# Four-layer graph network, 64 graphs: the plan's account of PSUM changed from half banks to whole banks, and the order made anew

## The chip, the cores and the metric

The kernel runs on one core of one Trainium2 chip. A core has a matrix engine (TensorE, PE in the profile, with its weight loads shown apart as PEld), three elementwise engines (VectorE = DVE, ScalarE = ACT, GpSimd = POOL) and a sync engine (SP), which here issues every DMA. Matrix products land in PSUM, of which this program holds eight tiles of 128 x 512 float32, one bank each. The metric is the device time of one execution in microseconds (us).

## The reference, cut to what matters

There are 64 graphs of 256 nodes with 256 features in float32. Each goes through four layers in turn, and after each layer `x = layernorm(x + layer(x, adj))`:

```
layer 0: X,q,k = leaky_relu(x@W) in 4 heads;  A = adj * sigmoid(q k^T), scaled by degree^-1/2 on both sides
         out = layernorm(A @ X)
layer 1: 8 heads of masked softmax attention, then @ Wo
layer 2: agg = eps*x + adj @ x;  h = silu(rmsnorm(agg @ W1 + b1))   (W1: 256 x 1024)
         out = h @ W2 + b2                                           (W2: 1024 x 256)
layer 3: Wh = x @ W;  softmax over masked leaky_relu(s1_i + s2_j);  out = gelu(layernorm(att @ Wh))
```

The graphs are independent of each other. Within a graph each layer waits for the one before.

## The kernel before, in words

The program is fully unrolled and its order is made by a planner written in Python, which runs while the kernel is built. `graph()` lists the work of one graph as operations (`op(engine, cost, fn, writes, reads, ...)`). A `Value` is a buffer; its letter says where it lives: `s`, `d`, `b`, `c` are SBUF buffers of several sizes, `h` lies in DRAM, and `p` is one PSUM bank. The slots of each kind are limited (`SLOTS`: 42 of `s`, 8 of `p`, and so on). A `Value` may have parts: most PSUM values have two, the two halves of the bank (columns 0 to 255 and 256 to 511). An operand written `(ps, 0)` names one half, a bare `ps` names all.

`Plan.order()` then schedules all operations of all 64 graphs against a table of costs. It picks, among the operations whose predecessors are placed, the one with the earliest start; ties go to the one that is due first. Three things besides data bear on the choice:

- `AHEAD`: an operation without predecessors (a load from DRAM) may be placed only when the current turn is within `AHEAD` turns of the turn in which its result is due. Turns are the stretches in which ScalarE keeps one table of functions; a graph passes four of them per round, and there are 272 in all.
- `STAY`: when PE has just run products that use a part of the array's rows or columns (`mode="rows"`: L444 and L524; `mode="columns"`: L462, L484 and L560), a candidate of another mode has its start raised by `STAY` nanoseconds in the comparison, so that PE stays in the mode while it can. Everything else is `full` or `transpose`.
- `CHANGE` and `AFTER`: the planner's own prices of a change of mode and of a hand-over between engines.

The operations are then emitted in the order of their planned starts (`emit`), and a layer below puts in the semaphores: an instruction waits for the earlier-emitted instructions whose buffers it touches. The planner's parts decide the order; they do not set the semaphores. Each engine runs its instructions strictly in the emitted order.

The names that the later sections use, with their lines in the kernel before: 

- L603: the hidden layer of layer 2. `agg` is multiplied with `W1`; each bank takes two operations on PE, one per half (`[(ps, i)]`), 256 banks in all. L608 and L610 are ScalarE's readers of each half: the square for the norm (`sq`) and the scaled copy (`hT`). L615 adds the squares on DVE.
- L645: the second product of layer 2; L591: the product with the adjacency; L637: its Silu.
- L320 and L331: the plain projections (`feature_major`, `token_major`), each two operations for a bank. The query projection of layer 1 is read half by half at L510 (ScalarE); the attention product of layer 3 (L331 `ps<-v,eT`) is read half by half by the statistics at L345 (DVE).
- L524: the scores of layer 1, four banks in one operation; L407 (DVE) and L412 (ScalarE) are their softmax. L444 to L484 are layer 0's scores, degrees and product.
- L545, L287 with L547, L549, L293 to L301: transposes through DRAM, issued on SP.

Of the kernel before, what the change touches and what calls it, by code (L numbers as in the profile page):

```python
# [27 lines left out]
DMA_KB, DMA_SEEN = 4, 1900  # L28

WORDS = {"s": 516, "d": 1024, "b": 2048, "c": 32, "p": 512, "h": 1024}  # L30
AHEAD = 14
STAY = 200
NEAR = 1, 1, 3

ROUND = 0, 2, 5, 7
# [43 lines left out]
class Plan:  # L79
# [7 lines left out]
        self.graph = 0  # L87

    def op(self, engine, cost, fn, w=(), r=(), turn=None, mode="full", after=None, size=0):
        pair = lambda x: x if isinstance(x, tuple) else (x, None)  # L90
        w, r = [pair(x) for x in w], [pair(x) for x in r]
        op = Op(engine, cost, fn, w, r, self.graph, turn, mode, after, size)
        op.table = turn is not None and engine == "ACT"
        if op.table:
            self.turns[turn] = self.turns.get(turn, 0) + 1
        self.ops.append(op)

    def order(self):
# [13 lines left out]
        while ready:  # L112
            best = None
            for op in ready:
                if (op.due - AHEAD if op.first else op.turn or 0) > turns[turn]:
                    continue
                start = clock[op.engine]
                if op.engine == "PE" and mode in ("rows", "columns") and mode != op.mode:
                    start += STAY - 60 * (op.mode == "transpose")
                start = max(start, op.ready)  # L120
# [15 lines left out]
            _, start, op = best  # L136
            op.start = start
            ready.discard(op)
            if op.table and op.turn != loaded:
                op.start, loaded = op.start + TABLE_LOAD, op.turn  # L140
# [5 lines left out]
            if op.engine == "SP":  # L146
                moved = max(moved, end) + op.size * DMA_KB
                op.landed = max(op.landed, moved + DMA_SEEN)
            self.busy[op.engine] += op.cost
            done.append(op)  # L150
            op.takes = [v for v in op.values if v.slot is None]
            for v in op.takes:
# [26 lines left out]
def weights(plan, nc, c, t):  # L179
# [10 lines left out]
    def weight(name, key, rows=D, cols=D):  # L190
        v = const(name, [P, rows // P, cols])
        op("SP", 420, lambda: nc.sync.dma_start(
            v.t, t[key].rearrange("(k p) f -> p k f", p=P)), [v], after=3500, size=rows * cols // 256)
# [580 lines left out]
```

## Time and profile before

| | us |
|---|---|
| median of 3 runs (2766.03 to 2769.21) | 2768.54 |
| the profiled execution | 2761.13 |
| its span, first to last instruction | 2759.3 |
| PE busy | 2703.5 |
| PEld busy | 2160.5 |
| DVE busy | 2443.0 |
| ACT busy | 2224.2 |
| POOL busy | 574.6 |

Busy times overlap between engines. A PE product of 128 x 256 is shown with 379 ns, but a stream of them starts one every 216 ns (the timeline has 32 of L603 in 7.17 us), so PE can be shown as busy while it stands behind its best pace by up to 163 ns. The granted clock was 0.996. A time "waited for" is idle time of the waiting engine ahead of an instruction, put down to the event that ended it.

### The profile page before, as it was taken

To read this page: it belongs to the slowest core of one execution; us is meant where nothing else is said; L and a number is where in the kernel's file an instruction comes from. 1 tells how busy PE (TensorE), PEld (TensorE's weight loads), DVE (VectorE), ACT (ScalarE), POOL (GpSimd) and SP (SyncE) were. 2 spreads that over 40 slices of the span, in tenths; PEclk is the share of its full clock that TensorE was granted. 3 is DMA by queue.
4 is the path that set the end of the run, shared out by engine and by line. 5 is a ranking of instruction groups with operands and counts; after the bars stand their busy time and mean duration, and the time that the engine had idled before them with its cause. 6 is when DMAs were issued, how large, how long until landed. Compare 5 with 4: busy or idle time off the path is not lost.

```text
span 2759.3 us, 56034 instructions
## 1 busy us (share of the span) xinstructions
PE 2703.5 (98%) x17280; PEld 2160.5 (78%) x17280; DVE 2443.0 (89%) x7426; ACT 2224.2 (81%) x5323; POOL 574.6 (21%) x902
## 2 busy tenths in 40 slices
PE   8999999999999999999999999999999999999997
PEld 6778777777777777787877877788778777777776
DVE  6989998898898889989989989889989899899966
ACT  4878888778788888788878887888888887888775
POOL 1112222122121121221221212212212122122212
PEclk9999999999999999999999999999999999999999
DMA  5677677676677566766756756757667677576651
GB/s 157 199 210 198 172 204 201 176 205 167 193 215 191 157 192 173 211 176 189 210 161 190 217 158 195 211 152 209 184 176 212 166 189 218 143 206 188 184 135 35
DMA packets 710923, 505.17 MB, mean 183 GB/s; under 512 B 310112, under 2 KB 669920, under 8 KB 710624
## 3 DMA queue, kind: packets, MB, share of 16 engines
q1 hardware_dynamic: 710624, 501.59, 65.9%
q8 instruction: 138, 2.26, 0.3%
q14 instruction: 161, 1.32, 0.2%
HBM read 303.44 MB, written 197.92 MB: 182 GB/s over the span
## 4 chain that ended last, share of the span: by engine, by line
PE 75%; DVE 10%; ACT 6%; DMA 4%; SPq 2%; issue 2%; POOL 0%; DVEq 0%; POOLq 0%; ACTq 0%
PE ps L331 13%; PE ps L320 13%; PE ps L645 13%; PE ps L603 11%; PE ps L444 4%; PE ps L524 4%; PE ps L484 3%; PE av L560 3%; PE ps L660 3%; PE ps L591 3%; ACT e L412 2%; DVE e L407 2%; DVE st L345 1%; DMA eT<-far 1%; PE ps L275 1%
## 5 line engine op out<-in xcount | busy, mean ns | idle before, releaser
L412 ACT ACTIVATE e<-e,low 128x256 f32<-128x256 f32 x1152 | 579.8, 505 | 87.5 <-DVE low L407 86.6
L645 PE MATMUL ps<-w,hT 128*128 128x256 f32 x2048 | 478.8, 383 | 5.5 <-ACT hT L637 4.8
L603 PE MATMUL ps<-aggT,w 128*128 128x256 f32 x2048 | 476.4, 382 | 3.8 <-DVE low L407 1.9
L357 POOL TENSOR_SCALAR mv<-mv 128x2 f32<-128x2 f32 x384 | 123.0, 320 | 1573.3 <-DVE mv L347 1012.1
L645 PEld LDWEIGHTS ps<-w,hT 128*128 128x128 f32 x2048 | 382.4, 191 | 68.1 <-issue 6.7
L603 PEld LDWEIGHTS ps<-aggT,w 128*128 128x128 f32 x2048 | 379.7, 190 | 69.4 <-DVE low L407 11.7
L407 DVE CUSTOM_DVE_ANT_0 e<-ps,adj 128x256 f32<-128x256 f32 x1024 | 361.1, 420 | 12.7 <-PE ps L524 11.2
L545 DVE STREAM_TRANSPOSE eb<-e 128x1024 f32<-128x1024 f32 x252 | 306.2, 1224 | 9.3 <-ACT e L412 9.2
L608 ACT ACTIVATE sq<-ps,b 128x256 f32<-128x256 f32 x512 | 242.0, 480 | 82.7 <-PE ps L603 73.0
L358 POOL TENSOR_TENSOR mv<-mv,mhalf 128x2 f32<-128x2 f32 x384 | 298.6, 778 | 32.0
L610 ACT ACTIVATE hT<-ps,br,r 128x256 f32<-128x256 f32 x512 | 288.8, 575 | 10.2 <-PE ps L645 6.7
L372 ACT ACTIVATE x<-y,mv 128x256 f32<-128x256 f32 x384 | 217.3, 602 | 50.9 <-DVE mv L368 48.9
L345 DVE BATCH_NORM_STATS2 st<-y 128x6 f32<-128x256 f32 x640 | 245.2, 413 | 0.9
L412 ACT ACTIVATION_READ_ACCUMULATOR e<-e,low 128x1 f32 x1152 | 225.4, 196 | 0.0
L615 DVE TENSOR_TENSOR sq<-sq 128x512 f32<-128x512 f32 x192 | 131.0, 682 | 98.1 <-ACT sq L608 97.2
L450 DVE TENSOR_TENSOR att<-att,adjT 128x512 f32<-128x512 f32 x256 | 166.6, 681 | 5.1 <-ACT att L448 5.1
L524 PE MATMUL ps<-kT,qT 32*128 32x256 f32 x2048 | 152.0, 400 | 4.3 <-ACT kT L311 4.2
L635 DVE TENSOR_TENSOR hT<-hT,pr 128x1024 f32<-128x1024 f32 x128 | 149.7, 1209 | 5.3 <-PE pr L631 5.3
L470 POOL TENSOR_TENSOR dp<-dp,mhalf 128x8 f32<-128x8 f32 x64 | 106.8, 1668 | 196.3 <-DVE dp L469 166.2
L448 ACT ACTIVATE att<-ps 128x512 f32<-128x512 f32 x256 | 132.2, 603 | 5.6 <-PE ps L444 3.0
L637 ACT ACTIVATE hT<-hT 128x1024 f32<-128x1024 f32 x128 | 128.9, 1050 | 9.1 <-DVE hT L635 7.9
L524 PEld LDWEIGHTS ps<-kT,qT 32*128 32x128 f32 x2048 | 97.9, 184 | 47.5 <-issue 23.3
(113 smaller groups left out, 5486.0 us busy)
## 6 DMA issues: line engine op xcount, KB each, us to landing
far<-eb SPq DMA_DIRECT2D x252, 512.0 KB, 3.8
eT<-far SPq DMA_DIRECT2D x1008, 128.0 KB, 3.9
adj<-in_adj SPq DMA_DIRECT2D x128, 256.0 KB, 4.6
far<-eb SPq DMA_DIRECT2D x488, 64.0 KB, 1.8
x0T<-in_xT SPq DMA_DIRECT2D x64, 256.0 KB, 3.6
adjT<-in_adjT SPq DMA_DIRECT2D x64, 256.0 KB, 4.4
x<-in_x SPq DMA_DIRECT2D x64, 256.0 KB, 4.8
adj<-in_adjT SPq DMA_DIRECT2D x64, 256.0 KB, 5.4
```

The costliest lines, as they stand in the source:

```text
L320: pe.matmul(two(ps)[:, o, :], w.t[:, k, o * P:(o + 1) * P], two(xT)[:, k, :], start=(k == 0), stop=(k == DB - 1))
L331: pe.matmul(two(ps)[:, n, :], two(xT)[:, k, n * P:(n + 1) * P], w()[:, k, :], start=(k == 0), stop=(k == DB - 1))
L345: op("DVE", 328, lambda n=n: dve.bn_stats(st.t[:, 6 * n:6 * n + 6], two(src)[:, n, :]), [(st, n)], [(src, n)])
L358: pool.tensor_tensor(m()[:, :, 2], m()[:, :, 2], c.mhalf[:, :NB], OP.pow)
L407: op("DVE", 345, lambda n=n: dve.tensor_tensor_reduce(out=E(n), in0=two(logits)[:, n, :], in1=two(negmask)[:, n, :], scale=-scale, scalar= ...
L412: op("ACT", 491, lambda n=n: act.activation(E(n), E(n), AF.Exp, bias=low.t[:, n:n + 1], scale=-1.0, accum_out=r.t[:, col(n):col(n) + 1]), ...
L524: pe.matmul(two(pss[i])[:, n, :], two(qT1)[s, hq, n * P:(n + 1) * P], two(kT1)[s, hq, :], start=True, stop=True)
L545: op("DVE", 1155, lambda e=e, eb=eb: dve.transpose(eb.t.rearrange("p (b g i) -> p g b i", b=4, i=32), e.t.rearrange("p (g b i) -> p g b i" ...
L603: pe.matmul(two(ps)[:, i, :], c.w2_1.t[:, k, (j + i) * P:(j + i + 1) * P], two(aggT)[:, k, :], start=(k == 0), stop=(k == DB - 1))
L608: op("ACT", 357, lambda ps=ps, sq=sq, i=i, j=j: act.activation(two(sq)[:, i, :], two(ps)[:, i, :], AF.Square, bias=c.b2_1.t[:, j + i:j + i ...
L610: op("ACT", 491, lambda ps=ps, i=i, j=j: act.activation(Hb(j + i)[:, 0], two(ps)[:, i, :], AF.Identity, bias=c.br2.t[:, j + i:j + i + 1], ...
L645: pe.matmul(two(ps)[:, n, :], Hb(j)[:, 0, n * P:(n + 1) * P], c.w2_2.t[:, j, :], start=(j == 0), stop=(j == HB - 1))
```

## The change

In the planner a part of a PSUM value no longer counts: an operand of kind `p` always stands for the whole bank. So in the plan a reader of either half comes after the products of both halves, and a product into the second half never comes after a reader of the first. Two constants go with it: `AHEAD` from 14 to 12, `STAY` from 200 to 250. `graph()` itself, the operations and the prices are the same; line numbers in the changed file are one higher from the edit on.

```diff
-AHEAD = 14
-STAY = 200
+AHEAD = 12
+STAY = 250
...
     def op(self, engine, cost, fn, w=(), r=(), turn=None, mode="full", after=None, size=0):
-        pair = lambda x: x if isinstance(x, tuple) else (x, None)
+
+        pair = lambda x: (x[0], None if x[0].kind == "p" else x[1]) if isinstance(x, tuple) else (x, None)
         w, r = [pair(x) for x in w], [pair(x) for x in r]
```

Because every choice of the planner depends on the ones before, the order of all five queues is new from near the start on. The number of instructions on each engine is the same in both.

## The prediction

> **What bounds the kernel now.** I read the head of the page first: which engine is full, and whose work the chain of waits is made of.
>
> ```profile
> span 2759.3 us, 56034 instructions
> PE 2703.5 (98%) x17280; PEld 2160.5 (78%) x17280; DVE 2443.0 (89%) x7426; ACT 2224.2 (81%) x5323; POOL 574.6 (21%) x902
> PE 75%; DVE 10%; ACT 6%; DMA 4%; SPq 2%; issue 2%; POOL 0%; DVEq 0%; POOLq 0%; ACTq 0%
> ```
>
> PE sets the end. DVE and ACT have slack, and count only where PE stands for them. So the question is how much PE stands, and where. The busy times by stretch (span, then PE, PEld, DVE, ACT, POOL) say where:
>
> ```profile
> 0.00:100.00 100.00, 92.27 (x618) 71.60 (x619) 68.02 (x203) 61.55 (x145) 15.48 (x24) 0.98 0.47 145
> ...
> 1300.00:1600.00 300.00, 298.12 (x1911) 239.37 (x1911) 268.39 (x816) 248.09 (x595) 61.51 (x98) 1.00 0.68 187
> ...
> 2620.00:2759.30 139.30, 114.25 (x602) 94.48 (x600) 91.86 (x279) 92.55 (x202) 26.21 (x49) 0.93 0.35 88
> ```
>
> PE is idle 55.8 us (2759.3 - 2703.5): 7.7 us in the first 100 us, 25.1 us in the last 139 us, of which 16.5 us follow its last product (the final norms). The 2520 us between hold only 23.0 us (the nine stretches there, with 2497.0 us busy). That is all a better order can show as idle in the steady state. Besides, PE loses time inside "busy" where products follow each other more slowly than every 216 ns, above all around the tiled modes. PE's timeline (start, duration) shows the price of one:
>
> ```profile
> 1486.78 1.89 PE L645 MATMUL ps<-w,hT 128*128 128x256 f32 x8
> 1488.60 2.00 PE L444 MATMUL ps<-qT,kT 64*128 64x256 f32 x16
> 1490.52 3.72 PE L645 MATMUL ps<-w,hT 128*128 128x256 f32 x16
> 1494.08 0.38 PE L669 MATMUL ps<-ident,v 128*128 128x128 f32 x2
> ```
>
> Going in: 1.82 us for eight products, against 8 x 0.216 = 1.73, is 0.09 more. The block takes 1.92 us where eight pairs at 0.216 make 1.73: 0.19 more. The 16 products after it take 3.56, against 3.46: 0.10 more. A lone tiled block thus costs 0.38 us over the bare products.
>
> Last, how the halves of a bank behave today. From the timelines of PE and ACT around one hidden layer:
>
> ```profile
> 103.05 7.07 PE L603 MATMUL ps<-aggT,w 128*128 128x256 f32 x32
> ```
>
> ```profile
> 104.98 0.47 ACT L608 ACTIVATE sq<-ps,b 128x256 f32<-128x256 f32 x1 [0.96 <-PE ps L603]
> ```
>
> Four instructions make a half. The first half was complete at about 104.1 (three pitches of 0.216 and one duration of 0.38), the whole bank at 103.05 + 7 x 0.216 + 0.38 = 104.94. ACT, idle for 0.96 us, started at 104.98: it waited for the **whole bank**, though it reads half. And the other way round:
>
> ```profile
> 448.55 0.48 ACT L608 ACTIVATE sq<-ps,b 128x256 f32<-128x256 f32 x1 [0.51 <-DVE xb L383]
> ...
> 449.28 0.57 ACT L610 ACTIVATE hT<-ps,br,r 128x256 f32<-128x256 f32 x1
> ...
> 449.90 1.99 PE L603 MATMUL ps<-aggT,w 128*128 128x256 f32 x8 [1.66 <-ACT hT L610]
> ```
>
> PE stood 1.66 us until ACT had read the first half, before it wrote the second. So the semaphores already keep a bank to one engine; only the planner thinks in halves.
>
> **What the Trainium skill says.** "PSUM — Partial Sum Buffer", section "PSUM bank collisions raise a hardware error", has two engines on one bank and the same partitions at once as an error, at different columns too, and the rule to guard by bank; the two waits above agree that this program is guarded so. "TensorEngine Tiling (Array Packing)", "Key Properties", says that a change of tiling mode drains TensorE; the 0.09 and 0.10 us above agree. "Perfetto Trace Analysis", "Identifying the Most-Contended Engine", warns that the busy share of products does not measure distance to the best; the 0.38 us hidden in a 100% busy stretch agrees.
>
> **The change part by part.** No instruction is added or removed (17280 on PE, and the same issues on SP); the order of all queues, SP's and POOL's among them, is new. I counted in the two orders.
>
> (a) Tiled blocks. `STAY` 250 keeps PE longer in a mode. Runs of L444/L524 fall from 182 to 173, runs of L462/L484/L560 from 115 to 105. A merged block saves the way in and the way out, 0.09 + 0.10, and at most the whole 0.38: 19 x 0.19 = 3.6 to 19 x 0.38 = 7.2 us, all on PE's path. I take **-4**.
>
> (b) Second halves placed behind a reader of the first: 21 banks before (17 of L603, 4 of L331), none after. At four of these places PE's pitch shows the loss: 1.83 us at 449.90, 0.29 at 670.03, 0.18 at 2556.35, 0.22 at 2667.07 (pitch less the usual one). **-2.5**, with 0 as the other bound, if PE then stands for the next thing.
>
> (c) Readers planned too early. At the other 239 banks of L603, the 64 of the query projection and 60 of layer 3 the plan starts the reader when half a bank is done; the real one stands for the other half, 0.86 us of products on. The waits of before show it on ACT and DVE:
>
> ```profile
> DVE sq L615 <- ACT sq L608: 97.2, 73, 4.6
> ACT e L412 <- DVE low L407: 86.6, 65, 4.8
> ACT sq L608 <- PE ps L603: 73.0, 72, 2.9
> ACT qT L510 <- PE ps L320: 24.5, 23, 3.2
> DVE st L345 <- PE ps L331: 23.5, 27, 2.5
> ```
>
> In the new order ACT has other work there. These 121 us (73.0 + 24.5 + 23.5) lie beside PE's work and are not 121 us of gain; they matter as far as late ACT and DVE work makes PE stand later. PE's middle idle time without (b) is about 21 us; by PE's list of waits most of it ends on ACT or DVE. I take a third of it, **-7**; bounds 0 and -21.
>
> (d) Banks held longer. A half no longer frees its reader, and other work slips between the halves more often: banks whose halves aren't adjacent on PE go from 209 to 273 (L603: 31 to 67). Such a bank stays taken meanwhile, and PE may find none of the eight free. The nearest row is L603 standing for DVE L407 (which frees banks): 13.6 us in 34 waits, 0.4 us each, and 0.16 hidden, 0.56. That hit 34 of 256 banks, 13%: 64 x 13% x 0.56 = 5; below, 0; if all 64 stood, 36. I take **+2**.
>
> (e) `AHEAD` 12. A turn is 2759 / 272 = 10.1 us, so a load is issued about 20 us later, still some 120 us ahead of use. Loads land in 3.6 to 5.4 us (the page's DMA issues): nothing, covered by the lead itself; on SP they now stand behind more of the transposes' issues. It frees `s` buffers (live ones in order of emission: peak 42 of 42 before, 41 after), so no load waits for a slot; too small to price.
>
> (f) Start and end. The first 28 PE operations are nearly the same, the last 40 nearly so, and the drain after them is the same chain: 0, with +-4 as bounds.
>
> Sum: -4 - 2.5 - 7 + 2 = -11.5 us. Against the profiled execution's own 2761.1 that is 2749.6. That execution was 7.4 us quicker than the median of the runs shown (2768.5), so on the median I expect **2757**.
>
> **The rivals.** *The stalls only move.* PE's waits (c) come from a greedy order's accidents and return elsewhere; only (a) stays, some of it spent on (d): -4 + 2, 2766.5. For it: PE idles only 23 us in 2520, and ACT's waits cost little now. Against: (b) is a plain loss that goes. Much the same holds if the edit doesn't do what it says: real banks were never shared, so nothing is protected that was not. *The banks become the bound, slower.* One mechanism: half-filled banks held across other work (d), with no gain from (c). If 30 of the 64 further split banks make PE stand 0.56 us, that is +16.8 against -6.5: +10.3, 2779. It decides from about 21 such waits on ((6.5 + 5.5) / 0.56). For it: DVE L407 ends already more of L603's idle time than any other releaser. Against: a split is chosen because another product was ready, so PE works meanwhile. *The plan now fits the machine.* All of the 21 us of (c) goes, with (a) and (b): -27.5, 2741. For it: ACT's and DVE's waits above are the model's error made visible. Against: PE also stands for transfers and for true chains.
>
> **How the numbers follow.** A measurement of this kernel can tell about 0.2%, 5.5 us, from no change. Likeliest case 0.48, with the larger gain 0.13: faster 0.61. Stalls only move: 0.16. Slower: 0.23. The range runs from 2736 (the large gain, with the upper bound of (a) and of (f)) to 2780 (the bank rival).
>
> **What would show it.** Right: ACT L608's wait for PE L603 falls from 73 us to below 25; no PE wait on ACT L610 ahead of an L603; about 253 instead of 279 ways from full or transpose into tiled products; PE's idle time between 100 and 2620 us near 14 instead of 23. Wrong: PE standing for DVE L407 well beyond the 13.6 us at L603 (then the banks bind), or PE idle as long as before while ACT's waits are gone (then they never mattered).

## The result, and the profile after

| | before | after |
|---|---|---|
| median of 5 runs each, us | 2766.7 (2763.5 to 2769.2) | 2746.95 (2742.6 to 2752.1) |
| the profiled execution, us | 2761.13 | 2746.95 |
| its span, us | 2759.3 | 2745.2 |

The ratio is 0.9928, with a 95% interval of 0.9912 to 0.9945: 19.75 us less in the medians. The two profiled executions differ by 14.2 us, because the one of before was a quick one.

The head of the page after:

```profile
span 2745.2 us, 55992 instructions
...
PE 2690.7 (98%) x17280; PEld 2172.4 (79%) x17280; DVE 2442.3 (89%) x7426; ACT 2222.4 (81%) x5323; POOL 567.8 (21%) x902
```

PE is idle for 2745.2 - 2690.7 = 54.5 us, against 55.8 before. Of the 14.1 us of span only 1.3 are idle time; 12.8 came out of PE's *busy* time, though PE runs the same 17280 products. So nearly all of the gain lies in time that the page shows as busy. The busy times by stretch (span, then PE and the other engines) say the same:

```profile
0.00:100.00 100.00, 90.63 (x585) 68.70 (x586) 63.10 (x187) 58.98 (x139) 14.21 (x22) 0.97 0.44 137
...
1300.00:1600.00 300.00, 297.82 (x1934) 239.75 (x1933) 272.62 (x836) 248.08 (x600) 62.63 (x98) 1.00 0.71 192
...
2605.90:2745.20 139.30, 115.11 (x606) 96.18 (x604) 90.71 (x282) 89.66 (x201) 25.82 (x50) 0.93 0.35 92
```

Start (9.4 us idle against 7.7) and end (24.2 against 25.1) are as before, and between 100 us and the last 139 us PE idles 21.0 us against 23.0. The waits of ACT and DVE that the change was to shorten (waiting engine and line, releaser, us, times, longest):

```profile
ACT e L413 <- DVE low L408: 75.8, 42, 4.0
DVE sq L616 <- ACT sq L609: 75.1, 63, 5.4
...
ACT qT L511 <- PE ps L321: 33.0, 25, 4.2
...
ACT sq L609 <- PE ps L604: 27.1, 46, 2.9
...
DVE st L346 <- PE ps L332: 9.2, 11, 2.0
```

Line numbers are one higher than before. ACT's wait for the hidden layer's banks fell from 73.0 to 27.1 us; the query projection's, which is the same kind of bank, rose from 24.5 to 33.0; DVE's for layer 3's attention product fell from 23.5 to 9.2. The three together fell from 121.0 to 69.3 us.

**What hides in "busy".** Two blocks of layer 1's scores in PE's timeline of the kernel before (start, duration):

```profile
128.15 1.15 PE L524 MATMUL ps<-kT,qT 32*128 32x256 f32 x16
129.22 0.28 PE L567 MATMUL ps<-ident,r 128*16 128x128 f32 x1
129.34 1.89 PE L331 MATMUL ps<-w_o,yT 128*128 128x256 f32 x8
131.16 1.56 PE L524 MATMUL ps<-kT,qT 32*128 32x256 f32 x16
132.66 1.99 PE L320 MATMUL ps<-x0T,w_q 128*128 128x256 f32 x8
```

The same 16 products took 1.07 us from start to the next start in one place and 1.50 in the other. No idle time is noted, since an instruction is always in flight. I therefore compared, for all 17280 products of each profile, the time to the next start with the pitch of that place in its block where nothing is waited for (the lower quartile over all profiles of this study). What lies next to or within tiled blocks at that best pace, over the bare products, I call modes; what is above it at any place, waits. The bare products make 2551.1 us in every kernel. Before: modes 91.2, waits 92.9. After: modes 90.4, waits 79.6. With a start of 6 to 7 us and 17 us from the last product's start to the end this adds up to the spans, to about 1 us.

By this split the waits fell by 13.3 us and the modes by 0.8. For a single pair of profiles the split is soft, though. If the places are told apart more or less finely, or a product that is quicker than its place's best pitch counts against the waits and not the modes, the same two traces give waits 6.5 to 16.7 us lower and modes between 8.4 us lower and 1.9 us higher. What these two profiles show is that idle time is not where the gain lies; which part is waits has to come from more pairs.

### The profile page after: what moved, and what is told of

It is laid out like the page before. It is cut to its first block, busy times and chain, and to the rows that moved or that the text cites. A ratio compares the mean times of both kernels' runs of the same rounds, so it can differ in the third digit from the quotient of the medians.

```text
span 2745.2 us, 55992 instructions
## 1 busy us (share of the span) xinstructions
PE 2690.7 (98%) x17280; PEld 2172.4 (79%) x17280; DVE 2442.3 (89%) x7426; ACT 2222.4 (81%) x5323; POOL 567.8 (21%) x902
## 5 line engine op out<-in xcount | busy, mean ns | idle before, releaser
L609 ACT ACTIVATE sq<-ps,b 128x256 f32<-128x256 f32 x512 | 239.4, 477 | 41.3 <-PE ps L604 27.1
L451 DVE TENSOR_TENSOR att<-att,adjT 128x512 f32<-128x512 f32 x256 | 166.7, 679 | 10.1 <-ACT att L449 10.1
L321 PE MATMUL ps<-x0T,w_q 128*128 128x256 f32 x512 | 130.1, 389 | 7.7 <-DMA x0T<-in_xT 6.7
```

What stands on the lines that cost most here:

```text
L321: pe.matmul(two(ps)[:, o, :], w.t[:, k, o * P:(o + 1) * P], two(xT)[:, k, :], start=(k == 0), stop=(k == DB - 1))
L609: op("ACT", 357, lambda ps=ps, sq=sq, i=i, j=j: act.activation(two(sq)[:, i, :], two(ps)[:, i, :], AF.Square, bias=c.b2_1.t[:, j + i:j + i ...
```

## The experiments

Theory A: the whole-bank rule itself pays, because the plan then counts with the waits that the semaphores impose. Theory B: the two constants pay, through fewer changes of mode. Theory C: any new order of this plan is a new draw within some 10 us, and the change had a good one. All ratios are to the kernel before, run on the same chip in the same session. Its median was 2770.5, 2764.1 and 2769.5 us in the three sessions, so between sessions ratios can be off by some 0.002, beyond their intervals. "Runs" of tiled products are maximal stretches of one kind.

**The rule alone.**

```diff
-        pair = lambda x: x if isinstance(x, tuple) else (x, None)
+        pair = lambda x: (x[0], None if x[0].kind == "p" else x[1]) if isinstance(x, tuple) else (x, None)
```

> The kernel before with the whole-bank rule alone (AHEAD 14, STAY 200). Counted in its order: 308 runs of tiled products in 300 stretches, against 297 in 279 before; no second half behind a reader. Theory A (the rule itself pays, because the plan now knows the real waits): most of the 20 us gain is here, 12 to 18 us faster, in spite of 11 more tiled runs (+2 to +4 us). Theory B (the two constants pay, by fewer mode changes): nothing or slower, -2 to +5 us. Theory C (any new order of this greedy plan lands within some 10 us of any other, and the change took a lucky one): anywhere from -10 to +10 us, and not the sum that the other parts would ask for.

Measured: 0.9977 (0.9968 to 0.9985), 2764.8 us against 2770.5. Faster by 6 us: half or less of what A asked for, more than B did, and within C.

**The constants alone.**

```diff
-AHEAD = 14
-STAY = 200
+AHEAD = 12
+STAY = 250
```

> The kernel before with the two constants alone (AHEAD 12, STAY 250), the plan still in half banks. Its order has 297 tiled runs in 287 stretches and 17 second halves behind a reader. Theory A: within 5 us of before. Theory B: 10 to 20 us faster, though its tiled runs did not become fewer. Theory C: from -10 to +10 us.

Measured: 1.0070 (1.0055 to 1.0085), 2791.4 us: slower by 21 us. B falls, and A and C had not allowed for so much either. The parts don't add: +21 and -6 would make +15, and the whole change is -20.

**The rule with one constant each.** Whole banks and `STAY = 250`, with `AHEAD = 14`:

> The changed kernel with AHEAD back at 14: whole banks, STAY 250. 301 tiled runs in 282 stretches. Theory A: 12 to 20 us faster than before. Theory B: about 10 us faster. Theory C: anywhere within 10 us of before or of the changed kernel, without order among the four.

Measured: 1.0028 (1.0019 to 1.0037), slower, where A and B had it faster. Whole banks and `AHEAD = 12`, with `STAY = 200`:

> The changed kernel with STAY back at 200: whole banks, AHEAD 12. 299 tiled runs in 275 stretches. Theory A: 12 to 18 us faster than before. Theory B: about 5 to 10 us faster. Theory C: no order among the four.

Measured: 0.9968 (0.9955 to 0.9980), 9 us faster: less than A asked for. The four whole-bank kernels, the changed one among them, run from 0.9928 to 1.0028 without an order that A or B foresaw, which looks like C. What was missing was the half-bank partner at each pair of constants.

**The partners in half banks.** The kernel before with `STAY = 250`:

> The kernel before (half banks, AHEAD 14) with STAY 250. 305 tiled runs in 296 stretches, 19 second halves behind a reader. Its partner with whole banks came out 1.0028 of before. Theory A (the rule pays on the whole, whatever the constants): slower than its partner by 5 us or more, 2784 us and up where before has 2770. Theory C (a new order is a new draw, within some 15 us to either side): no telling, 2755 to 2790.

Measured: 1.0071 (1.0056 to 1.0086). With `AHEAD = 12`:

> The kernel before (half banks, STAY 200) with AHEAD 12. 309 tiled runs in 298 stretches, 17 second halves behind a reader. Its partner with whole banks came out 0.9968 of before. Theory A: at least 5 us above its partner, 2767 us and up where before has 2770. Theory C: no telling, 2755 to 2790.

Measured: 1.0097 (1.0080 to 1.0115). Both lie above their partners, as A has it.

**A step of 10 ns in one constant.** The changed kernel with

```diff
-STAY = 250
+STAY = 260
```

> The changed kernel with STAY 260 in place of 250, a step too small to mean anything for the machine. Its order is nevertheless new: 322 tiled runs in 304 stretches, against 278 in 253. Theory A: within 5 us of the changed kernel, 2745 to 2755 us where before has 2768, apart from 44 more tiled runs at 0.2 to 0.4 us, which would add 9 to 17 us. Theory C: the changed kernel was a good draw, and this one lies 10 to 25 us above it, 2757 to 2775 us, through its waits as much as its modes.

Measured: 1.0040 (1.0025 to 1.0055), 2774.5 us. A step of 10 ns in the planner's comparison does nothing on the chip but give it another order, and that order is about 1% slower than the changed kernel, above what A allowed for, and somewhat above C's 10 to 25 us as well. A single order says little. Its modes are 101.7 us, its waits 96.6, against 90.4 and 79.6: the waits make more of it. And the partner in half banks:

> Half banks with AHEAD 12 and STAY 260: the partner of the whole-bank kernel with the same constants, which gave 1.0040. At four other pairs of constants whole banks were ahead each time, by 0.0023 to 0.0142. Theory A (the rule pays on the whole): 1.006 or more. Theory C (a draw): as likely below 1.004 as above.

Measured: 1.0142 (1.0118 to 1.0166), again above. Together, with the two worked-out terms of each profile:

| AHEAD, STAY | half banks: ratio, modes, waits | whole banks: ratio, modes, waits | rule |
|---|---|---|---|
| 14, 200 | 1 (before), 91.2, 92.9 | 0.9977, 100.0, 88.3 | -0.0023 |
| 14, 250 | 1.0071, 99.9, 107.0 | 1.0028, 93.3, 107.7 | -0.0043 |
| 12, 200 | 1.0097, 101.3, 112.2 | 0.9968, 98.2, 81.8 | -0.0129 |
| 12, 250 | 1.0070, 99.0, 112.4 | 0.9928 (after), 90.4, 79.6 | -0.0142 |
| 12, 260 | 1.0142, 96.7, 139.6 | 1.0040, 101.7, 96.6 | -0.0102 |

Whole banks win in all five rows, by 0.0088 on average, 24 us; the one at 14, 250 compares two sessions and is not far above what those differ by. The means of the profiles say where (that of before was a quick one, 6 us under the median above, so its waits are on the low side): modes 97.6 against 96.7 us, waits 112.8 against 90.8. Here the ways to split agree: 22 to 24 us on the waits, under 2 us on the modes. **On the mean of five pairs the rule works through time that PE loses in waits, some 22 us; the modes take next to no part.** Within a column the orders scatter by 0.011 to 0.014, more than the rule is worth. The kernel before was the best of its column, the changed one the best of the other.

Two more readings of the same ten kernels say what kind of waits these are. The first is the finish that the planner itself expects (`self.span` in `Plan.order()`, from each kernel's planner run alone). The second is the readers' waits of the prediction's part (c), the three rows added up: ACT for the hidden layer and for the query projection, DVE for layer 3's attention product.

| AHEAD, STAY | half banks: plan's finish, readers' waits | whole banks: plan's finish, readers' waits |
|---|---|---|
| 14, 200 | 2703.4, 121.0 | 2719.9, 97.1 |
| 14, 250 | 2719.1, 151.3 | 2721.8, 100.5 |
| 12, 200 | 2717.7, 155.0 | 2707.0, 86.7 |
| 12, 250 | 2711.3, 137.3 | 2707.2, 69.3 |
| 12, 260 | 2728.1, 191.2 | 2726.2, 90.5 |

The plans of the two columns finish at the same time on average (2715.9 and 2716.4), and that of the changed kernel finishes 3.8 us later than that of before. But the measured medians lie 63 to 80 us above the plan with half banks and 40 to 57 us with whole ones, without overlap. So the rule doesn't make a better plan; it makes the plan truer. The readers' waits fall in every pair. And part of the scatter is no draw: of the 27.5 us between the medians at `STAY` 260 and 250 (from two sessions) the plan itself has 19.0.

A rival for the waits is TensorE's clock. The traces have stretches of 3.4 or 6.8 us in which it was granted at 0.5, and products of 256 columns then start every 427 ns in place of 216. Between 100 us and the last 139 us of the span these stretches add up to 19.8 us on average with half banks (none in the profile of before) and 14.3 with whole ones. Half of the difference, 3 us, is the most that the clock can have of the 22. Whether a stand of PE brings such a stretch on was not tried.

How such a wait term looks on the page, by the two kernels with `AHEAD = 12, STAY = 260`, half banks first:

```profile
span 2810.5 us, 56141 instructions
...
PE 2727.9 (97%) x17280; PEld 2171.7 (77%) x17280; DVE 2443.8 (87%) x7426; ACT 2224.6 (79%) x5323; POOL 605.4 (22%) x902
```

```profile
span 2772.0 us, 56178 instructions
...
PE 2704.1 (98%) x17280; PEld 2161.5 (78%) x17280; DVE 2440.2 (88%) x7426; ACT 2223.4 (80%) x5323; POOL 592.1 (21%) x902
```

38.5 us of span: 14.7 as idle time (82.6 against 67.9), 23.8 as a busier PE. DVE and ACT do the same work in the same time. In this pair the clock has a larger part than on the mean: 41.0 us at 0.5 in the first trace and 17.1 in the second, up to 12 us of the difference.

**Which banks.** The rule for the hidden layer's 256 banks alone, and for all others alone, at `AHEAD = 12, STAY = 250`; the hidden layer's banks are told apart by a name, and the complement has `!=` in place of `==`:

```diff
-        pair = lambda x: (x[0], None if x[0].kind == "p" else x[1]) if isinstance(x, tuple) else (x, None)
+        pair = lambda x: (x[0], None if x[0].kind == "p" and x[0].name == "hid" else x[1]) if isinstance(x, tuple) else (x, None)
...
-        ps = Value("p", "ps", 2)
+        ps = Value("p", "hid", 2)
```

> AHEAD 12 and STAY 250 as in the changed kernel, the whole-bank rule for the 256 banks of the hidden layer (L603) alone. With the rule for none the same constants gave 1.0070 of before, with it for all 0.9928, a difference of 39 us. 300 tiled runs in 291 stretches. If the hidden layer, which has most of the readers planned too early (239 of 363), carries the rule: 0.993 to 0.999. If it is the other banks: 1.004 or more. If orders only scatter: in between, and not to be told apart.

Measured: 1.0023 (1.0013 to 1.0033).

> The complement: the same constants, the whole-bank rule for all banks but those of the hidden layer. 313 tiled runs in 304 stretches. If the hidden layer carries the rule: 1.004 or more. If the other banks do: 0.993 to 0.999. If both this one and its complement come out well above 0.9928, the parts don't add up and the order of the changed kernel owes part of its time to a good draw.

Measured: 1.0099 (1.0080 to 1.0119). None, hidden layer, others, all: 1.0070, 1.0023, 1.0099, 0.9928. By the ratios the hidden layer alone brings a third of the gap and the others alone nothing; the rest comes only with both, and given the scatter the ratios can't be split further. Measured against each one's own plan the order is clearer: the medians lie 80.1, 55.2, 71.5 and 39.8 us above the plan's finish, so the hidden layer carries more than half. The traces agree: each partial rule shortens the waits of its own readers only. ACT's wait for the hidden layer is 72.1 us with the rule for none, 50.7 with the hidden layer alone and 71.9 with the others alone; DVE's for layer 3's attention product is 25.1, 26.0 and 10.1.

**The interlocks by themselves.** The order of before, in which only the 21 products that stood behind a reader of the other half are emitted ahead of it:

```diff
...
+                early = [place[r] for r in v.everyone if r.engine != "PE" and place[r] < place[op]]
+                if early:
+                    move[op] = min(early) - 0.5
+    return sorted(ops, key=lambda op: move.get(op, place[op]))
...
-    for op in plan.order():
+    for op in whole_banks(plan.order()):
```

> The order of before, with one thing changed: the 21 products of a second half that stood behind a reader of the first half are emitted just ahead of that reader; everything else keeps its place, so the readers of the other banks are still planned too early. If step (b) of the prediction has the right size: 2 to 4 us faster than before, 0.9985 to 0.9993. If the interlocks only hid other waits: no difference. If they are most of the rule's gain: over 5 us.

Measured: 1.0036 (1.0022 to 1.0050), 2774.1 us: slower by 10 us than the kernel before in the same session, and by 3.6 to 7.4 us than its medians elsewhere. What ended PE's idle time ahead of the hidden layer's products, and in the last line who waited for them, in the trace before and then in this one:

```profile
  DVE low L407: 13.6, 34
  ACT hT L610: 5.4, 6
...
  ACT sq L608: 73.0, 72
```

```profile
  DVE low L409: 13.1, 33
...
  ACT hT L612: 1.2, 3
...
  ACT sq L610: 89.8, 80
```

The interlock did go (5.4 to 1.2 us) and the stands for banks stayed, but ACT's wait for the hidden layer's banks rose by 16.8 us: what PE no longer stood, the reader stood, since it now had to wait for the second half. (Its profile has 105.1 us of waits on PE, but that can't be set against the 92.9 of before: the next kernel's profile has 104.2 with a median like before's.) As a counterpart, 21 other second halves, none interlocked, moved up behind their first halves:

> The order of before with 21 other second halves moved up right behind their first halves, none of which stood behind a reader, so no interlock is taken away; tiled runs stay 297 in 279 stretches. A counterpart to the run in which the 21 interlocked halves were moved and which came out 10 us slower. If any small disturbance of a tuned order costs about that much: 1.002 to 1.005. If it was something about the interlocked places: within 0.001 of before.

Measured: 0.9995 (0.9983 to 1.0007). ACT's wait for the hidden layer stayed at 70.9 us here. So moving 21 halves costs nothing by itself. It is not quite a like for like, as most of these are projections (13 of L331, 3 of the hidden layer), where in the run before 16 of the 18 halves that passed another product were the hidden layer's (the other three of the 21 moved only against other engines' work). What costs the time there is open. Mostly L320 products had stood between the halves, and a half moved ahead of them delays them by its four instructions, 0.86 us; the reader's longer wait is another candidate. The two were not moved apart. Nor can the profile place it: it is 10.3 us behind that of before by 950 us and 11.1 at the end, while 14 of the 18 places come after. Shown is only that taking the interlocks out of an otherwise unchanged order brings no gain.

## Why the prediction was right, point by point

The direction and the size hold: 11.5 us expected, 14.2 between the profiled executions, 19.75 in the medians. 2746.95 lies about halfway between the likeliest case (2757) and the one with the larger gain (2741). The core of the account, readers planned too early, is what the five pairs and the two partial rules bear out. The terms hold less well, and that their sum came near is in part luck: nothing in (b) to (d) depends on the constants, yet with 14, 250 and 12, 260 whole banks came out at 1.0028 and 1.0040, slower than before.

- **(a) Modes, -4: size open.** The count was right, 279 ways into tiled products became 253. By the split above the term measured -0.8 us, by others -8.4 to +1.9; 26 ways in and out at the prediction's own 0.19 would be -4.9. Nor does `STAY` 250 as such make the runs fewer: 297 to 305 and 309 to 297 with half banks, 308 to 301 and 299 to 278 with whole ones, and 322 at 260. The low count belongs to this order.
- **(b) Interlocks, -2.5: failed.** The waits at the four places were read nearly rightly (at 2556.35 the usual pitch after such a transpose is 0.11, so 0.29 was lost and not 0.18), and the 21-halves run took such waits away; no time came back. The stated other bound, 0, was already too hopeful for that edit by itself. The sign "no PE wait on ACT L610" was met nearly: 1.0 us in 2 times. It is not a clean sign, as two other whole-bank kernels, which have no interlocks, show 4.5 and 6.1 us.
- **(c) Readers planned too early, -7: right mechanism, too small, and looked for in the wrong place.** The rule's mean over five pairs is 24 us where (b), (c) and (d) made -7.5. The term was sized as a third of PE's visible idle time; between 100 us and the last 139 us that fell by 2.0 us, and the rest of the gain came out of busy time. The forecast that ACT's wait for the hidden layer would fall below 25 us was nearly met (27.1); that PE's middle idle time would be near 14 us was not (21.0). By the prediction's own sign of being wrong, PE idle nearly as long as before while ACT's waits shrink, these waits would never have mattered; the sign missed because it looked at idle time only. ACT's wait for the hidden layer alone is no measure of the gain either: it is 54.9 us with whole banks at 14, 250, well below before, and that kernel is slower. The three readers' waits together do fall in each pair, and they rank the half-bank kernels as their times do.
- **(d) Banks held longer, +2: wrong sign.** The halves do lie apart more often in this order (209 to 273 banks), though not by the rule: in the other four whole-bank orders it is about 200 to 220, and in the half-bank ones 210 to 235. And what ends PE's idle time ahead of the hidden layer after reads

```profile
  DVE low L408: 5.6, 15
```

against 13.6 us in 34 times before. Fewer stands for a free bank, not more, and so in all five pairs (10.8 against 6.6 us on average). That a plan which knows when a bank really comes free places its next user better is my reading of it. The rival that banks become the bound falls with it.
- **(e) `AHEAD`, 0:** with whole banks at `STAY = 200` it moved the ratio by -0.0009, within the intervals. At `STAY = 250` it moved it by -0.0001 with half banks, but by -0.0100 with whole ones, more than the changed kernel's whole gain. With half banks at 200 it cost 0.0097. An effect of both signs looks like another order each time and not like loads; with half banks at 200 the waits are what differs (92.9 to 112.2), and PE's largest wait for a load is the first one in both traces, 6.1 and 6.0 us. So I take it for the order.
- **(f) Start and end, 0:** right, within 2 us. (The range's lower end is 2734 by the terms that it names, not 2736.)

The rival "the stalls only move" falls: over five pairs of constants they became fewer each time but at 14, 250 (107.0 and 107.7), where the modes fell instead.

## What to carry to other kernels

Let the planner's model have the rule that the semaphores keep. A plan that allows what they forbid (here, half a bank at a time) looks no worse by its own account, and the few spots where it is plainly wrong were not where the time could be got back; it shows in the distance between plan and measurement, which was 72 us with half banks and 49 with whole ones. So compare that distance, too. Judge such a rule over several neighbouring orders, each with its partner: a 10 ns step in one constant moved this kernel by 1.1%, more than the rule's mean. And where the matrix engine is near 100% busy, sum the times between starts, not the idle gaps, over several pairs of profiles.

## What the runs showed of the hardware

- One bank that comes free late can cost a block of four concurrent row tiles its whole wait, though the other tiles go on. In the block at 131.16 us the third and fourth tile's first products started at 131.59, 0.43 us after the first two (in an undisturbed block all four start within 0.02 us). The third tile's first product waits for a semaphore of DVE, and starts 0.06 us after the end of this step in DVE's timeline of the kernel before:

```profile
131.11 0.42 DVE L407 CUSTOM_DVE_ANT_0 e<-ps,adj 128x256 f32<-128x256 f32 x1
```

The two pairs then ran through the block out of step: 1.50 us in place of 1.07, the same 0.43 us, and no idle time in the profile.
- One profile is one draw of the run time too. The run with the 21 other halves had a median of 2767.7 us and a profile of 2774.1. Product by product it was 10.3 us behind the profile of before by 950 us, and for the next 700 us the distance stayed within 0.5 us: the difference arose in the first third and was carried along. At most 3.4 us of it is the clock, which was at 0.5 for 3.4 us at 145 and again at 937 us and nowhere in the first third after 100 us in the profile of before. What makes the rest vary was not tried.
